# A Mamba layer and a position-attention layer: silu of z applied when the gate is loaded, a new order for the first image, and other shares of the scan's products for ScalarE, VectorE and GpSimd

## The chip, the cores and the metric

The kernel runs on one core of one Trainium2 chip. The metric is the device time of one execution in microseconds (us). Before the change it was measured three times: 3,081.79, 3,085.72 and 3,090.05 us, with a median of 3,085.72 us. One more execution was profiled, and its trace is read here.

A core has five engines, each with its own queue of instructions: TensorE (PE in the profile; its weight loads are PEld), VectorE (DVE), ScalarE (ACT), GpSimd (POOL) and SyncE (SP), which here only starts transfers between the chip's main memory (DRAM) and the on-chip memory. Matmuls write into PSUM[...], here used in tiles of 128 x 512 float32.

## What is computed

Input x is 4 x 512 x 32 x 32 in float32. Two layers follow each other. The first is a Mamba layer on the group-normalised x, with 1,024 inner channels, 16 states for each, and 1,024 time steps for each of four images:

```python
xz = xn @ W_in
xm, z = (xz[..., :d_inner], xz[..., d_inner:])
xc = jax.lax.conv_general_dilated(xm.transpose(0, 2, 1), conv_w[:, None, :], (1,), [(D_CONV - 1, 0)], ...)
xs = jax.nn.silu((xc + conv_b[None, :, None]).transpose(0, 2, 1))
proj = xs @ W_x
dt = jax.nn.softplus(proj[..., :dt_rank] @ W_dt + b_dt)
Bm = proj[..., dt_rank:dt_rank + D_STATE]
Cm = proj[..., dt_rank + D_STATE:]
A = -jnp.exp(A_log)

def step(h, inp):
    dt_t, B_t, C_t, x_t = inp
    dA = jnp.exp(dt_t[..., None] * A)
    h = dA * h + (dt_t * x_t)[..., None] * B_t[:, None, :]
    y = jnp.einsum('bds,bs->bd', h, C_t)
    return (h, y)
...
y = ys.transpose(1, 0, 2) + xs * D_param
y = y * jax.nn.silu(z)
out = y @ W_out
```

Here xn is the layer-normalised input. The result is added to x. The second layer group-normalises that sum again and computes two 1x1 convolutions (64 channels each), a softmax over their 1,024 x 1,024 products, a 3x3 convolution with 512 channels weighted by that softmax, and another 3x3 convolution with 512 channels. Its result is added too. All is float32.

## The kernel before

**Layer 0, units and groups.** Channels lie on the 128 partitions, time along the row. A *unit* is one state s of one pair of channel chunks (e, 256 channels) in one half of the time (h, 512 steps) of one image (b). Sixteen units make a *group*, eight groups an image, and there are 32 groups. For each unit (`unit`, line 814 on):

- ScalarE computes the decay exp(dt * A), line 832, two calls of 128 x 512.
- dt * x * B is formed in one of two ways. For s in `B_ON_ACT` (nine of sixteen) ScalarE scales the transposed dt * x by B (`sc`, line 844, four calls of 128 x 256) and TensorE transposes the result back into the PSUM ring `u` (line 870, eight transposes). For the other seven, GpSimd multiplies by a B row that a transfer has spread over the partitions (`dbx`, line 859, 128 x 1024).
- VectorE runs the scan along time (line 884, two of 128 x 512), and in the first half of the time stores the last state (line 889).
- The state is multiplied by C: on GpSimd (line 906, 128 x 1024), or for s in `C_ON_DVE` (four of sixteen) on VectorE (line 900, two of 128 x 512).
- TensorE adds the product over s, transposed, into y (line 913, eight instructions).

A group begins with `delta` (dt with its softplus, line 785; dt * x on GpSimd, line 793) and ends with `gate`: ScalarE copies y out of PSUM (line 936), TensorE turns it back, VectorE adds D * x and multiplies by silu(z).

**What lies between the groups.** The next image is prepared inside the groups of the present one: `norms` (statistics and normalisation), `conv1` (input projection, first tap on ScalarE line 639, three more on VectorE line 648, silu line 657), `gates` (projection of z, its silu at line 711, then a store to DRAM; `gate` loads it again), `params` (B, C and the input of dt), and `out_proj` of the image before. `transform`, called 32 times, turns the weights of the two 3x3 convolutions into the form that layer 1 uses: 12 additions on GpSimd each (lines 1173 to 1193), two scalings on ScalarE and 12 stores. For the first image `norms(0)` and `conv1_half` come before everything: the convolution is made half by half, with the last three columns of the first half kept in `tails` for the second (lines 676, 682, 687).

**What sets the order.** Nothing in layer 0 is issued where it is written. Each piece of work is recorded as a `Step` with its engine, an estimated duration, its reads and writes, a priority in units (`prio`), the activation table it needs (`table`), and the buffers that it takes from rings (`slots`: four `u` banks, four `h`, four `dbx` and so on). `Plan.issue` (line 106) keeps a clock for each engine, picks the step that can start first, breaks near ties by priority, charges 1.3 us (`LOAD`) when a step's table isn't the one loaded, and calls the step's function, which emits the instructions. So each engine has a fixed order, and priorities such as `PRM["dl"]` (how many units ahead `delta` comes), `m0`, `q0`, `c0`, `g0` or `tg` (distance of the transforms) decide it. The tables themselves are not loaded by the kernel: an instruction that needs another table gets a load (ACT_TABLE_LOAD) ahead of it when the kernel is compiled. Layer 0 has tables "exp", "ln", "silu" and "softplus".

**The end of layer 0 and layer 1.** The last image's gated y stays on chip; `last_proj` adds its output projection in parts, the last part after the last group. `first_image` loads image 0 for layer 1 and normalises it. Layer 1 is written in order: `scores` (matmuls `pt`, line 1324, and `psc`, line 1345), `conv3` (matmuls `m_b` and `m_o`, line 1468, whose operands `v` VectorE forms in lines 1453 to 1456 from `rr`), `attend` (matmuls `pat`). A scheduler chooses here in which order matmuls of different parts stand on TensorE.

## Time and profile before

| what | value |
|---|---|
| median of three runs | 3,085.72 us |
| the profiled execution | 3,085.98 us |
| its span, first to last instruction | 3,084.2 us |
| granted TensorE clock, mean | 0.967 |
| end of group 0 (its y copied, line 936) | 241.9 us |
| end of groups 7, 15, 23, 31 | 667.0, 1,147.6, 1,629.6, 2,044.5 us |
| first matmul of layer 1 (line 1324) | 2,058.3 us |

The profile gives for each engine the time in which it was busy, the idle time before groups of instructions, and what ended it (the releaser, an arrow). A table of windows gives, for stretches of the span in microseconds: their length, the busy time of TensorE's matmuls, of its weight loads, of VectorE, ScalarE and GpSimd (each with the number of instructions), the granted TensorE clock, the busy share of the transfer engines, and GB/s. The group view gives for each line of the program the count, the busy time in us, the mean duration in ns, and the idle time before. A line of the timeline begins with the start and the duration in us. A float32 matmul shows as two records, one per pass.

From 0 to 100 us VectorE is busy for 36.6 us and ScalarE for 40.0. Over the 32 groups every engine is busy for some nine tenths of the time. From about 2,060 us on layer 1 runs, in which TensorE is busy for 958.3 of the 984 us from 2,100 to 3,084.

### The profile page before, as it was taken

The page shows a single profiled execution, that of the slowest core. Times are in us where ns is not written, and L with a number is a line of the kernel's source. Part 1 is how long each engine was busy: PE and PEld are TensorE (multiplying, and loading weights), DVE is VectorE, ACT ScalarE, POOL GpSimd, SP SyncE. Part 2 cuts the span into 40 slices and gives each one's busy share as a digit, 9 for nine tenths or more (in the row PEclk, how much of TensorE's full clock was granted, in tenths as well). Part 3 has the DMA queues.
Part 4 walks back from the last instruction along what each step waited for, and adds up shares of the span by engine and source line. Part 5 has one row for each costly group of instructions (what it writes and reads, how often), then busy time and mean ns, then how long its engine had stood idle before and what let it go on. Part 6 is the DMA issues. An engine that isn't in the chain of part 4 may idle for free. (4 is left out here: it accounts for less than half of the span.)

```text
span 3084.2 us, 36053 instructions
## 1 busy us (share of the span) xinstructions
PE 2760.5 (90%) x11512; PEld 1625.3 (53%) x11512; DVE 2325.2 (75%) x3021; ACT 1864.1 (60%) x3218; POOL 2181.5 (71%) x1221
## 2 busy tenths in 40 slices
PE   4788789999879999879999978779999999999998
PEld 2245556656656666656656656544444444444444
DVE  3567999989999988999999899986275375447344
ACT  4578899998789999779999787741120030021000
POOL 6899988899988899998899999862151142224222
PEclk8899899999989999988999999999999999999999
DMA  6776645578745567755557755638178448628827
GB/s 170 216 208 197 178 143 164 171 210 255 230 138 163 165 204 238 236 176 158 174 167 238 237 184 151 148 123 307 54 259 314 163 165 315 256 76 313 309 86 259
DMA packets 410292, 610.49 MB, mean 198 GB/s; under 512 B 47832, under 2 KB 246744, under 8 KB 385528
## 3 DMA queue, kind: packets, MB, share of 16 engines
q1 hardware_dynamic: 401296, 593.67, 61.1%
q10 hardware_dynamic: 8648, 14.26, 1.3%
q8 instruction: 92, 1.51, 0.2%
q14 instruction: 96, 0.79, 0.1%
q0 software_dynamic: 160, 0.26, 0.0%
HBM read 511.09 MB, written 96.99 MB: 197 GB/s over the span
## 5 line engine op out<-in xcount | busy, mean ns | idle before, releaser
L906 POOL TENSOR_TENSOR da<-da,cbc 128x1024 f32<-128x1024 f32 x288 | 680.6, 2370 | 80.4 <-DVE da L884 50.7
L844 ACT ACTIVATE sc<-dtxt,bt_sb 128x256 f32<-128x256 f32 x1152 | 506.6, 497 | 70.6 <-PE u L870 70.1
L859 POOL TENSOR_TENSOR dbx<-dtx,bbc 128x1024 f32<-128x1024 f32 x224 | 529.1, 2373 | 20.1 <-PE y L913 7.0
L832 ACT ACTIVATE da<-dt,a_sb 128x512 f32<-128x512 f32 x576 | 395.4, 712 | 45.7 <-PE y L913 42.9
L884 DVE TENSOR_TENSOR_SCAN da<-da,carry_sb,u 128x512 f32<-128x512 f32 x288 | 357.6, 1263 | 34.5 <-PE u L870 34.5
L870 PE MATMUL u<-ident,sc 128*128 128x128 f32 x2304 | 345.8, 284 | 41.1 <-DVE da L884 26.0
L913 PE MATMUL y<-ident,da 128*128 128x128 f32 x2304 | 317.3, 282 | 53.2 <-POOL da L906 50.7
L913 PEld LDWEIGHTS y<-ident,da 128*128 128x128 f32 x2304 | 269.3, 145 | 155.6 <-POOL da L906 104.5
L884 DVE TENSOR_TENSOR_SCAN da<-da,u 128x512 f32<-128x512 f32 x288 | 348.6, 1210 | 2.6 <-PE u L870 2.4
L1468 PE MATMUL m_b<-uw_b,v_b 128*128 128x512 f32 x768 | 336.3, 595 | 8.8 <-DMA uw_b<-u_b 7.7
L870 PEld LDWEIGHTS u<-ident,sc 128*128 128x128 f32 x2304 | 277.2, 146 | 122.8 <-DVE da L884 34.7
L1468 PE MATMUL m_o<-uw_o,v_o 128*128 128x512 f32 x768 | 334.2, 595 | 4.3 <-DVE v_o L1387 4.1
L832 ACT ACTIVATE u<-dt,a_sb 128x512 f32<-128x512 f32 x448 | 297.6, 680 | 47.3 <-DVE da L884 27.6
L913 PE MATMUL y<-ident,dbx 128*128 128x128 f32 x1792 | 267.8, 289 | 61.2 <-DVE dbx L900 31.0
L913 PEld LDWEIGHTS y<-ident,dbx 128*128 128x128 f32 x1792 | 219.2, 149 | 135.0 <-issue 48.0
L394 PE MATMUL pxm<-xt,winc 128*128 128x345 f32 (+3 forms) x704 | 249.4, 498 | 29.3 <-DMA winc<-in_w_in_dram 12.9
L394 PE MATMUL pz<-xt,winc 128*128 128x512 f32 x512 | 240.3, 601 | 8.4 <-ACT sz L707 2.1
L1468 PEld LDWEIGHTS m_b<-uw_b,v_b 128*128 128x128 f32 x768 | 143.2, 190 | 195.0 <-issue 174.5
L1468 PEld LDWEIGHTS m_o<-uw_o,v_o 128*128 128x128 f32 x768 | 145.3, 190 | 190.1 <-issue 181.3
L906 POOL TENSOR_TENSOR dbx<-dbx,cbc 128x1024 f32<-128x1024 f32 x96 | 227.2, 2366 | 15.5 <-DVE dbx L884 7.5
L1518 PE MATMUL pat<-y_b,st 128*128 128x512 f32 x512 | 221.7, 593 | 0.1
L1476 ACT ACTIVATE e_b<-m_b 128x512 f32<-128x512 f32 x24 | 14.3, 597 | 307.9 <-PE m_b L1468 306.3
(233 smaller groups left out, 4543.1 us busy)
## 6 DMA issues: line engine op xcount, KB each, us to landing
cbc<-bcd SPq DMA_DIRECT2D x512, 256.0 KB, 3.7
uw_b<-u_b SPq DMA_DIRECT2D x96, 1024.0 KB, 5.1
uw_o<-u_o SPq DMA_DIRECT2D x96, 1024.0 KB, 4.8
bbc<-bcd SPq DMA_DIRECT2D x224, 256.0 KB, 3.9
u_b<-work SPq DMA_DIRECT2D x192, 128.0 KB, 2.7
u_o<-work SPq DMA_DIRECT2D x192, 128.0 KB, 3.3
winc<-in_w_in_dram SPq DMA_DIRECT2D x72, 256.0 KB, 3.6
szd<-sz SPq DMA_DIRECT2D x32, 512.0 KB, 4.1
```

The lines of the kernel that those rows point to most:

```text
L394: lambda k=k, lhs=lhs, rhs=rhs: nc.tensor.matmul(p()[:, at : at + cols], lhs(), rhs(), start=(k == 0), stop=(k == n - 1)),
L832: nc.scalar.activation(t, dt()[:, j], AF.Exp, scale=a_sb[:, at : at + 1])
L844: nc.scalar.activation(sc()[:, k], dtxt()[:, k], AF.Copy, scale=bt[:, at, s : s + 1])
L859: lambda: nc.gpsimd.tensor_mul(hc(), dtx(), b_bc().to_broadcast([P, 2, T])),
L870: nc.tensor.transpose(u()[:, k * P : (k + 1) * P], sc()[:, k, j, :], ident)
L884: nc.vector.tensor_tensor_scan(ht, *((hc()[:, j], u()) if on_act else (u(), hc()[:, j])), carry_sb[:, j, s : s + 1] if h else 0.0, ALU.mul ...
L906: lambda: nc.gpsimd.tensor_mul(hc(), hc(), c_bc().to_broadcast([P, 2, T])),
L913: nc.tensor.matmul(y[j]()[:, k, :], hc()[:, j, k * P : (k + 1) * P], ident, start=(s == 0 and k == 0), stop=(s == NS - 1 and k == NK - 1), ...
L1468: nc.tensor.matmul(m[q], v[:, q, k, c, :], w[:, c, :], start=(c == 0), stop=(c == NCC - 1 and not extra),)
L1476: nc.scalar.activation(e, m[2], AF.Copy, scale=al / 2)
L1518: nc.tensor.matmul(pt, st[m][:, 2 * P * j + h : 2 * P * (j + 1) : 2], xb[m // 2][:, m % 2, :], start=(m == 0), stop=(m == NMC - 1),)
```

## The change

The change has several parts, all in layer 0 and its order:

1. **silu of z.** `gates` stores z as it is. The silu is applied when the gate is loaded (`load_gate`, on the tile `szl`), inside the step that computes the softplus of the next group: `delta` takes a list `jobs`, whose functions are called before the softplus. The silus of the next image's convolution join the same list, two chunks at a time. So a group has one visit to the silu table, one to the softplus table, and then the exponential's again. `gate` of a group is recorded after `delta` of the next (`end_group`).
2. **Tables.** Ln, which had a table of its own in the plan, shares the exponential's: `exp_set` loads a set that has both, by hand, whenever the plan goes back to "exp".
3. **The first image.** x is loaded before anything else except one small matrix; the two halves are normalised one after the other, with more buffers for the squares; `conv1_half` and its `tails` are replaced by `conv1_first`, which uses the same `conv_part` as the other images and projects three columns of the first half again. The transforms come after the first projections by priority.
4. **Shares of the products.** Ten B products of sixteen go by ScalarE and TensorE, eleven in the last image. In the last image VectorE makes two C products instead of four, and GpSimd the others.
5. **Distances.** `dl` 10.28 to 8.5, `t0` 11 to 7 and `tg` 21.42 to 18.5 (the transforms), `m0`, `e0` and the convolution of image 1, and the new `zl` and `f1`.

```diff
-PRM = dict(..., m0=45.7, n0=50.77, nl=2.05, q0=65.56, qg=5.2, ..., e0=3.46, ..., dl=10.28, t0=11, tg=21.42)
+PRM = dict(..., m0=48, n0=50.77, nl=2.05, ..., e0=6, ..., dl=8.5, t0=7, tg=18.5, zl=11.5, f1=1.5)
...
-            s.fn()
             if late:
                 t += self.LOAD
                 table = s.table
+                if table == "exp":
+                    self.exp_set()
+            s.fn()
...
+    def exp_set():
+        nc.scalar.preload_act_table_set("natural_log_exp_and_others")
+
+    exp_set()
...
+        first_x = xtp.tile([P, NCC, L], F32, tag="xt", name="xt_0", bufs=1)
+        for c in range(NCC):
+            nc.sync.dma_start(first_x[:, c, :], x[0, c * P : (c + 1) * P].rearrange("p h w -> p (h w)"))
...
-        B_ON_ACT = (0, 2, 4, 6, 8, 10, 12, 14, 15)
-        C_ON_DVE = (1, 5, 9, 13)
+        B_ON_ACT = [(0, 2, 4, 6, 7, 8, 10, 12, 14, 15)] * (B - 1) + [(0, 2, 3, 4, 6, 8, 10, 11, 12, 14, 15)]
+        C_ON_DVE = [(1, 5, 9, 13)] * (B - 1) + [(5, 13)]
...
+            at_half = [prio + (lag * h if b else 0.5 * h) for h in range(NH)]
...
+                    if b:
+                        sq = buf("res", [P, T], f"sq_{b}_{h}_{c}")
+                        sqt = lambda sq=sq: sq()
+                    else:
+                        if c % 2 == 0:
+                            sq = buf(("dt", "dtx")[h], [P, 2, T], f"sq_{b}_{h}_{c}")
+                        sqt = lambda sq=sq, c=c: sq()[:, c % 2]
...
+        def silu(b, ds, hs=slice(0, L)):
+            hh = [h for h in range(NH) if hs.start < T * (h + 1) and hs.stop > T * h]
+            def each():
+                for d in ds:
+                    u = xs[b, d]()[:, hs]
+                    nc.scalar.activation(u, u, AF.Silu, bias=cb_sb[:, d : d + 1])
+            return (
+                each, len(ds) * (0.1 + 0.94 * len(hh) / NH), [xh[b, d][h] for d in ds for h in hh],
+                [xs[b, d] for d in ds],
+            )
...
+        def conv1_first(d, h, prio):
             if h == 0:
                 new_xs(0, d)
...
+            w = load_win(0, d, prio)
+            for at, end in (((0, T),), ((T, 768), (768, L)))[h]:
+                conv_part(0, d, w, at, end, prio, h == 0)
...
-            step(
-                "ACT", 0.97, lambda: nc.scalar.activation(sz(), sz(), AF.Silu),
-                [], [sz], prio, "silu",
-            )
...
-        def delta(b, e, h, prio):
+        def delta(b, e, h, prio, jobs=()):
...
+            def softplus():
+                for fn, *_ in jobs:
+                    fn()
+                nc.scalar.activation(dt(), dt(), AF.Softplus)
...
+        def load_gate(b, e, h):
+            prio = (b * NDC + 2 * e + h) * NS + NS
+            hs = halves[h]
+            sz = szl[b, e, h] = buf("szl", [P, 2, T], f"szl_{b}_{e}_{h}")
+            step(
+                "SP", 0.3, lambda: nc.sync.dma_start(sz(), szd[b][e][:, :, hs]),
+                szds[b][2 * e : 2 * e + 2], [sz], prio - PRM["zl"], kb=512,
+            )
+            return lambda: nc.scalar.activation(sz(), sz(), AF.Silu), 1.0, [sz], []
...
-            transform(u, src, k % NPC, -190 if k < PRM['t0'] else PRM['tg'] * (k - PRM['t0']))
+            transform(u, src, k % NPC, -5 if k < PRM['t0'] else PRM['tg'] * (k - PRM['t0']))
...
+                jobs = []
+                if b or n > 1:
+                    prev = b * NDC + n - 1
+                    jobs.append(load_gate(prev // NDC, prev % NDC // NH, prev % NH))
+                if b + 1 < B and n > 4:
+                    jobs.append(silu(b + 1, (2 * n - 10, 2 * n - 9)))
+                delta(b, e, h, at + n * NS - PRM["dl"] if b or n else -15, jobs)
+                end_group()
```

## The prediction

> **What bounds the kernel now.** I read the engine totals of the page first, then a table of windows, cut at the moments at which ScalarE copies a finished group's y (line 936), because the kernel is a chain of 32 such groups with a tail.
>
> ```profile
> PE 2760.5 (90%) x11512; PEld 1625.3 (53%) x11512; DVE 2325.2 (75%) x3021; ACT 1864.1 (60%) x3218; POOL 2181.5 (71%) x1221
> ```
>
> No engine stands out over the whole span, so the stages have to be looked at alone. The windows (us, busy PE, PEld, DVE, ACT, POOL):
>
> ```profile
> 0.00:100.00 100.00, 60.21 (x124) 24.85 (x124) 36.63 (x65) 40.04 (x67) 74.80 (x82) 0.90 0.64 179
> 200.00:241.90 41.90, 33.31 (x178) 22.08 (x177) 37.31 (x53) 36.20 (x64) 41.90 (x20) 0.94 0.61 183
> 721.06:777.69 56.63, 51.70 (x282) 35.98 (x280) 51.82 (x54) 45.07 (x86) 53.42 (x31) 0.97 0.84 261
> 894.56:968.31 73.75, 61.88 (x316) 44.22 (x315) 69.64 (x111) 67.79 (x110) 61.21 (x31) 0.93 0.50 150
> 1032.28:1096.24 63.96, 59.44 (x312) 38.97 (x311) 61.12 (x94) 62.36 (x107) 59.33 (x34) 1.00 0.60 176
> 1200.75:1259.02 58.27, 53.63 (x281) 36.34 (x279) 50.97 (x54) 47.27 (x86) 57.50 (x34) 0.94 0.82 266
> 1996.52:2044.48 47.96, 33.84 (x206) 24.56 (x207) 47.82 (x54) 25.49 (x50) 33.84 (x15) 0.96 0.52 139
> ```
>
> Three stages. Up to 241.9 us the first group is made; the vector engines idle most of the first 100. Then 31 groups take 1,802.6 us (2,044.5 - 241.9). In groups 1 to 3 of a batch POOL is full (57.5 of 58.3); in groups 5 to 7, where the next batch's convolution is interleaved, ACT and DVE are (62.4 and 61.1 of 64.0); at the very end DVE is (47.8 of 48.0). From 2,050 on layer 1 is TensorE's. The timeline of the start and of the crossing into layer 1:
>
> ```profile
> 24.00 0.16 DVE L476 SCALAR_TENSOR_TENSOR gnb_l<-gmean_l,pv_l 128x4 f32<-128x4 f32 x1 [2.47 <-ACT pv_l L463]
> ...
> 62.05 15.97 PE L394 MATMUL pxm<-xt,winc 128*128 128x512 f32 x32 [11.48 <-DMA winc<-in_w_in_dram]
> ...
> 114.89 2.49 POOL L793 TENSOR_TENSOR dtx<-dt,xs 128x512 f32<-128x512 f32 x2
> ...
> 2068.37 13.97 PE L1345 MATMUL psc<-center,top 128*128 128x512 f32 x32 [1.31 <-issue]
> ...
> 2075.77 1.25 DVE L1453 TENSOR_TENSOR v_b<-rr_b 128x1024 f32<-128x1024 f32 x1
> ```
>
> The statistics of the first image reach DVE at 24.00, after 2.47 us on ScalarE's Ln and Exp. The first projection (pxm) starts only at 62.05: before that TensorE waits 11.48 us for a weight load that stands behind transform stores on SP's queue. The first dtx is at 114.89. The table loads, by the groups view:
>
> ```profile
> L832 ACT ACT_TABLE_LOAD x76 | 97.5, 1283 | 1.4
> L785 ACT ACT_TABLE_LOAD x32 | 41.1, 1283 | 0.6
> L711 ACT ACT_TABLE_LOAD x28 | 35.9, 1283 | 0.5
> L657 ACT ACT_TABLE_LOAD x24 | 30.8, 1283 | 3.3 <-DVE xs L648 2.6
> ```
>
> **What the Trainium skill says.** "ScalarE: Activation LUTs", section What ACT_TABLE_LOAD costs, gives about 1283 ns for the load and about 1380 ns of drain on top. The trace has the 1283 ns, but the softplus load at 251.82 begins 0.01 us after the exponentials and the softplus 0.02 us after the load: no drain shows, so I price a load at 1.283 us. Its section Table sets: the hidden batching unit says that natural_log_exp_and_others has both exp and ln; no row of before shows it (Ln and Exp have a load each, lines 458 and 463). "PSUM — Partial Sum Buffer", section Engine vs sequencer instructions: queues are strict FIFO, and matmuls start in program order; the trace agrees (pxm above waits and everything behind it too). This carries the last part below.
>
> **The change, part by part.** Counts are from the order of the built programs.
>
> Table loads: 189 to 111, since silu of z moves into the step of the softplus of the next group, silus of the convolution join it, and Ln shares the exponential's set. 78 x 1.283 = 100 us less on ACT. Ten (last batch eleven) B products instead of nine: 40 more units on ACT, 160 sc activations. Alone they take 497 ns, back to back 0.44 (four in 1.71): +70 to +80 us. So ACT keeps 20 to 30 us, but the loads go mostly from groups 5 to 7 (28 loads in 894.56 to 1096.24, 3.2 groups, about 9 per group, against 3 after), where ACT binds; the products come everywhere.
>
> POOL: 40 B products fewer, 16 C products more (last batch four to two on DVE: 2 x 8). -24 x 2.37 = -57 us. DVE: 32 products fewer, 32 x 0.675 = -22 us, all in the last batch, and the little tail taps (line 687, 20.6 us) go in group 0. PE: 320 transposes more (four in 0.44): +35 us, nowhere the largest engine.
>
> Steady state. I counted, for each group and engine, the work that stands in program order between two group ends, with durations from the rows (issue to issue: POOL product 2.33, scan 1.235, sc 0.44, exp 0.63, load 1.283, matmul of 512 columns 0.86, four transposes 0.44), and took the largest engine of each group. For before this gives, for groups 1 to 7 of batch 0 and then batches 1, 2, 3: 419.3 + 472.4 + 472.6 + 425.6 = 1,789.9 us, and the trace has 425.1 + 480.6 + 482.0 + 414.9 = 1,802.6: within 1%. So the model may be used. For after: 413.0 + 463.5 + 465.0 + 428.0 = 1,769.5. The difference, **-20 us**, is small because the next engine is close: in the sixth and seventh group of batch 1 ACT falls from 62.3 and 64.1 to 54.8 and 56.3, but DVE stays at 60.7 and 59.2. In the last batch POOL takes over (its 2 x 8 more C products eat its saved B products, and four transforms instead of three lie there). The sums over all 31 groups say the same: largest engine 1,696 (DVE) before, 1,678 (POOL) after. What it could cost: the joined silu and softplus now hold ACT in one piece: 3 x 1.283 + 2 x 1.06 = 6.0 us, with two conv silus (1.15 each) 8.3 us, where a softplus alone took 3.6 us. Behind it stand the exponentials and sc of the next units, and the four u banks carry DVE over two units (5 to 7 us). Bounds: 0 lost to 20 lost; I take 0 beside the -20, since in before all waits of scans for exponentials (lines 884 after 832) came to about 27 us in 32 groups.
>
> Start. Five edits act together. x is loaded first: stats end about 3 us earlier, but a_sb (ready at 18.1, its multiply stands in DVE's queue) leaves some of it; Ln and Exp lose a load: mw about 3.6 us earlier. The halves go one after the other: the first half's mean takes 8 matmul passes (0.61 each, 4.9) instead of 16, then 2.7 (DVE), squares and variance to about 37.8, Ln and Exp 1.2, scaling 2.7 and affine 0.7: first projection at about 43 instead of 62.05, with winc already loaded. Eight projections at about 4 us and the eight parameter matmuls: proj copy at about 83 (100.4 before); copies, softplus with its load: 89.5. POOL has five transforms ahead of dtx (12.2 us each from about 21.4, with waits for ACT's scaling in between): dtx at 90 to 96 instead of 114.9. From there POOL still has 4 x 12.2 + 18 x 2.33 + 2.5 = 93 us up to the end of group 0 (113 before, which took 124.5 with its waits). With 11 to 13 us of waits: 95 + 105 = about 198 against 241.9. **-44 us**, bounds -30 (winc waits on SP, group 0 waits more) and -57 (no new waits). The three transforms that group 0 no longer holds (12 to 9) are in the steady sums already.
>
> Layer 1. Its order stays, but for one thing: the first matmul of m_b0 now stands before psc in TensorE's queue. It needs v_b's first plane, made by line 1453, which ends at 2077.0; psc started at 2068.37. FIFO then holds psc back. In after the output projection is no longer split by pt, so v_b comes 1.7 us earlier against it: 2077.0 + 0.9 - 1.7 - 68.4 = **+8 us**; bounds +3 (if the two rr_b sums, 3.6 us each beside POOL and 1.29 alone in other rounds, run fast) and +10. Layer 1's own Ln and Exp loads (6) lie where ACT idles: 0, hidden by the pat matmuls.
>
> Sum against the profiled execution's own 3,086.0 us (span 3,084.2), which is the median shown (3,085.7) within 0.3: 3,086 - 44 - 20 + 8 = **3,030 us**.
>
> **Rivals.** (B) The joined blocks take back the steady gain: 3,086 - 44 + 8 = 3,050. For: they are twice as long. Against: ACT has 3 to 8 us of slack per group after. (C) More than that: with ACT relieved the groups lose their 1% over the largest engine (13 us), group 0 waits 6 us less, and v_b is early (+3): 3,086 - 50 - 33 + 3 = 3,006. (D) Slower: one mechanism, DVE and POOL run dry behind each joined block. The place is ACT's queue at each softplus, 31 times, the price the excess over 3.6 us: 22 x 2.4 + 9 x 4.7 = 95 us; 3,030 + 95 = 3,125. It decides once a block starves the others for (44 + 20 - 8)/31 = 1.8 us. Against it: u and h rings carry two units, and projections and copies lie around. (E) The start doesn't gain, because POOL's transforms, not x, set it: 3,086 - 10 - 20 + 8 = 3,064. Against: the 11.48 us wait for winc and 16 passes in the way are real.
>
> **How the numbers follow.** Likeliest 3,030: 0.58, own range 3,015 to 3,045. B 0.17, C 0.12, E 0.06, D 0.06, no change 0.01. 0.3% of the time, 9 us, is about what a measurement of this kernel can tell from no change. Faster: 0.58 + 0.17 + 0.12 + 0.06 = 0.93, less a little of E: 0.92; slower 0.06; same 0.02. The range 3,000 to 3,060 holds the first three and leaves out D, E and the outer bounds.
>
> **What would show it.** First pxm near 43, proj near 83, first y copy near 198; 111 table loads; groups 5 to 7 of batches 1 and 2 at 60 to 62 with DVE full and ACT at 55; the last batch near 415 with POOL full; psc waiting about 8 us behind an m_b matmul that waits for v_b. Wrong if scans wait for exponentials for over 50 us in all, or if the first y copy stays beyond 215.

## The result, and the profile after

The changed kernel takes 3,077.7 us (median of 18 runs, 3,073.0 to 3,088.5), the kernel before, measured beside it, 3,079.8: a ratio of 0.9992, with a 95% interval from 0.9983 to 1.0001. No change is clear of the noise; 3,030 was predicted. The profiled execution has a span of 3,077.3 us. Cut at the same moments as before (ScalarE's copy of a finished group's y, now line 948), it divides as follows:

| stretch | before, us | after, us | change | predicted |
|---|---|---|---|---|
| up to the end of the first group | 241.9 | 198.0 | -43.9 | -44 |
| 31 groups | 1,802.6 | 1,835.0 | +32.4 | -20 |
| last y copy to the end (layer 1) | 1,039.7 | 1,044.3 | +4.6 | +8 |

The start and layer 1 came as worked out. The 31 groups in the middle should have become 20 us shorter and became 32 us longer: 53 us are missing there. The page's engine totals and the chain that ended last:

```profile
PE 2789.0 (91%) x11896; PEld 1669.4 (54%) x11896; DVE 2290.1 (74%) x2989; ACT 1822.0 (59%) x3300; POOL 2125.4 (69%) x1197
...
PE 40%; DVE 12%; ACT 6%; DMA 4%; POOL 4%; issue 3%; SPq 0%; DVEq 0%; POOLq 0%; ACTq 0%
```

VectorE, ScalarE and GpSimd all have less work than before (2,325.2, 1,864.1 and 2,181.5 us then), and TensorE has 28.5 us more. So for those three the amount of work doesn't explain the longer groups. The chain doesn't settle it either: it can be followed back over 69% of the span here, and before only over 44%. The granted TensorE clock was the same in the 31 groups, 0.96 before and after. The table loads did what was said (76 + 32 + 28 + 24 on the four lines shown before, with the rest 189; now 41 + 32 + 32 + 6):

```profile
L206 ACT ACT_TABLE_LOAD x41 | 52.6, 1283 | 3.1 <-issue 1.7 <-PEq L1681 0.7
L786 ACT ACT_TABLE_LOAD x32 | 41.1, 1283 | 0.5
L935 ACT ACT_TABLE_LOAD x32 | 41.1, 1283 | 0.5
L675 ACT ACT_TABLE_LOAD x6 | 7.7, 1283 | 1.9 <-DVE xs L661 1.9
```

The table of windows of after (stretch; us, busy PE, PEld, DVE, ACT, POOL with counts; granted clock, DMA share, GB/s): the fifth to eighth group of batch 1 and the fourth group of the last batch (a batch is an image).

```profile
859.42:931.68 72.26, 63.46 (x324) 44.02 (x323) 69.55 (x109) 63.72 (x112) 56.52 (x33) 0.98 0.49 138
931.68:996.57 64.89, 59.95 (x326) 41.82 (x325) 58.47 (x73) 53.38 (x98) 55.98 (x33) 1.00 0.56 167
996.57:1059.47 62.90, 57.27 (x314) 40.30 (x313) 60.55 (x95) 54.75 (x96) 58.88 (x34) 1.00 0.58 176
1059.47:1115.95 56.48, 56.24 (x299) 33.23 (x298) 45.11 (x48) 51.12 (x97) 49.66 (x30) 1.00 0.68 196
1771.17:1834.30 63.13, 41.09 (x248) 30.98 (x247) 44.21 (x43) 48.23 (x91) 59.45 (x35) 0.84 0.52 164
```

In the sixth group (64.89 us) nothing is full: DVE has 58.47, PE 59.95. The same view of before, for the sixth and the eighth group of batch 1 (the seventh stands in the prediction), has ACT close to full in the sixth and PE full in the eighth:

```profile
968.31:1032.28 63.97, 58.48 (x309) 41.59 (x308) 60.18 (x75) 61.35 (x101) 53.07 (x29) 0.95 0.57 161
1096.24:1147.56 51.32, 51.32 (x282) 32.75 (x282) 44.32 (x47) 48.02 (x83) 49.32 (x28) 1.00 0.65 198
```

ScalarE lost 8 us in the sixth and in the seventh group (61.35 to 53.38, 62.36 to 54.75), as predicted, and the groups lasted 0.9 us more and 1.1 us less. Idle time took the place of the work. Much of it shows in VectorE's waits, between the end of the first group and the last y copy (waiting line, what it waited for: us in total, times, longest). First of before, then of after:

```profile
DVE da L884 <- PE u L870: 36.9, 33, 3.1
DVE dbx L884 <- ACT u L832: 17.8, 16, 2.4
...
DVE da L889 <- PE u L875: 62.5, 35, 13.2
DVE dbx L889 <- ACT u L837: 50.1, 15, 7.5
```

In each pair the first line is a scan that waits for dt * x * B, transposed by TensorE, and the second one that waits for a decay in u (below: VectorE's wait for u). The prediction had set a mark here: wrong if scans wait for exponentials for over 50 us. Counted over all lines in which a scan waits for one, as the prediction had counted its 27 us, it is 26.7 us before and 56.2 after. One such wait in full, the timeline of after in the sixth group of batch 1 (start, us, engine, line, operation, in square brackets the idle time ahead and its releaser):

```profile
963.86 1.28 ACT L935 ACT_TABLE_LOAD   x1
965.15 1.06 ACT L935 ACTIVATE szl<-szl 128x1024 f32<-128x1024 f32 x1
966.12 2.17 ACT L675 ACTIVATE xs<-xs,cb_sb 128x1024 f32<-128x1024 f32 x2
968.31 1.28 ACT L786 ACT_TABLE_LOAD   x1
969.60 1.06 ACT L786 ACTIVATE dt<-dt 128x1024 f32<-128x1024 f32 x1
970.57 0.89 ACT L849 ACTIVATE sc<-dtxt,bt_sb 128x256 f32<-128x256 f32 x2
971.37 0.56 ACT L709 COPY sz<-pz 128x512 f32<-128x512 f32 x1
971.83 0.91 ACT L849 ACTIVATE sc<-dtxt,bt_sb 128x256 f32<-128x256 f32 x2
972.64 0.57 ACT L709 COPY sz<-pz 128x512 f32<-128x512 f32 x1
973.23 1.28 ACT L206 ACT_TABLE_LOAD   x1
974.52 1.30 ACT L837 ACTIVATE u<-dt,a_sb 128x512 f32<-128x512 f32 x2
...
975.25 2.46 DVE L889 TENSOR_TENSOR_SCAN dbx<-u,carry_sb,dbx 128x512 f32<-128x512 f32 x2 [4.84 <-ACT u L837]
```

From the first load at 963.86 to the next decay (the exponential of dt) at 974.52 are 10.66 us. The prediction had priced 8.3: it had left out that the plan sets table-free work (sc, copies of z) between softplus and the load back to the exponential, which lengthens the time without decays by 2.4 us. VectorE has nothing to scan from 970.41 on and stands for 4.84 us. I call such a time, from the first table load away from the exponentials to the next decay, a *stretch*; it is added up below from each kernel's ScalarE timeline over the 31 groups.

### The profile page after: what moved, and what is told of

It reads as the page before. It is cut to its first block, busy times and chain, and to the rows that moved or that the text cites. A ratio compares the mean times of both kernels' runs of the same rounds, so it can differ in the third digit from the quotient of the medians.

```text
span 3077.3 us, 36921 instructions
## 1 busy us (share of the span) xinstructions
PE 2789.0 (91%) x11896; PEld 1669.4 (54%) x11896; DVE 2290.1 (74%) x2989; ACT 1822.0 (59%) x3300; POOL 2125.4 (69%) x1197
## 4 chain that ended last, share of the span: by engine, by line
PE 40%; DVE 12%; ACT 6%; DMA 4%; POOL 4%; issue 3%; SPq 0%; DVEq 0%; POOLq 0%; ACTq 0%
PE m_o L1503 10%; PE m_b L1503 8%; PE pat L1553 7%; DVE da L889 5%; PE y L918 3%; PE po L402 2%; PE psc L1380 2%; PE u L875 2%; DMA uw_b<-u_b 2%; POOL da L911 2%; DVE dbx L889 2%; DVE u L889 1%; PE pz L402 1%; PE pp L728 1%; ACT sc L849 1%
## 5 line engine op out<-in xcount | busy, mean ns | idle before, releaser
L911 POOL TENSOR_TENSOR da<-da,cbc 128x1024 f32<-128x1024 f32 x328 | 773.2, 2368 | 114.7 <-DVE da L889 53.1
L849 ACT ACTIVATE sc<-dtxt,bt_sb 128x256 f32<-128x256 f32 x1312 | 578.1, 499 | 99.3 <-PE u L875 98.5
L837 ACT ACTIVATE da<-dt,a_sb 128x512 f32<-128x512 f32 x656 | 454.1, 716 | 78.8 <-PE y L918 62.8
L864 POOL TENSOR_TENSOR dbx<-dtx,bbc 128x1024 f32<-128x1024 f32 x184 | 434.4, 2373 | 10.6 <-DVE carry_sb L894 4.6
L918 PE MATMUL y<-ident,da 128*128 128x128 f32 x2624 | 366.6, 284 | 72.1 <-POOL da L911 69.9
L889 DVE TENSOR_TENSOR_SCAN da<-da,u 128x512 f32<-128x512 f32 x328 | 397.9, 1213 | 31.0 <-PE u L875 29.0
L402 PE MATMUL pxm<-xt,winc 128*128 128x341 f32 (+4 forms) x768 | 251.0, 470 | 21.7 <-DVE xs L661 10.5
L837 ACT ACTIVATE u<-dt,a_sb 128x512 f32<-128x512 f32 x368 | 245.5, 681 | 11.9 <-DVE da L889 6.7
L918 PE MATMUL y<-ident,dbx 128*128 128x128 f32 x1472 | 215.4, 285 | 36.0 <-DVE dbx L905 24.7
L661 DVE SCALAR_TENSOR_TENSOR xs<-pxm,cw_sb,xs 128x341 f32<-128x341 f32 (+8 forms) x288 | 163.6, 569 | 60.6 <-ACT xs L652 53.6
```

Of the source, the lines that this page charges most:

```text
L402: lambda k=k, lhs=lhs, rhs=rhs: nc.tensor.matmul(p()[:, at : at + cols], lhs(), rhs(), start=(k == 0), stop=(k == n - 1)),
L661: nc.vector.scalar_tensor_tensor(u()[:, first:end], p()[:, first - k - at + before : n - k + before], cw[k], u()[:, first:end], ALU.mult, ...
L837: nc.scalar.activation(t, dt()[:, j], AF.Exp, scale=a_sb[:, at : at + 1])
L849: nc.scalar.activation(sc()[:, k], dtxt()[:, k], AF.Copy, scale=bt[:, at, s : s + 1])
L864: lambda: nc.gpsimd.tensor_mul(hc(), dtx(), b_bc().to_broadcast([P, 2, T])),
L889: nc.vector.tensor_tensor_scan(ht, *((hc()[:, j], u()) if on_act else (u(), hc()[:, j])), carry_sb[:, j, s : s + 1] if h else 0.0, ALU.mul ...
```

## The experiments

Theory 1, after the first reading: the long stretch starves VectorE and, through it, the others. Its rivals: the new shares cost the time (2), the parameter products pile up in the last group of a batch (3), the transforms that left the first group are just paid back later (4). Times are medians; ratios are to the kernel before, measured beside each on the same chip. Stretches, waits and the lengths of groups are from the profiled execution.

### First four: undo one part each

**e1_conv_alone.** The silus of the convolution leave the joined block:

```diff
-                if b + 1 < B and n > 4:
-                    jobs.append(silu(b + 1, (2 * n - 10, 2 * n - 9)))
...
-                    alone(silu(b + 1, range(6, NDC)), at + PRM["c0"] + PRM["cg"] * NDC)
...
             for at, end in ((0, 341), (341, 682), (682, L)):
                 conv_part(b, d, w, at, end, prio)
+            alone(silu(b, (d,)), prio)
```

> The changed kernel with the convolution silus of batches 1 to 3 taken out of the blocks in front of softplus: each stands alone after its own channel group, as before; silu of z stays joined. Groups 5 to 8 of batches 0 to 2 took 777.8 us in the changed kernel (755.5 before). Theory 1, the long joined block starves VectorE and TensorE: those twelve groups come to about 755, VectorE's scans wait for u under 25 us in all instead of 50, and the time falls to about 3,055. Theory 2, the shares (ten B products, last batch) cost it: nothing returns, 3,078 plus up to 24 table loads of 1.28 us, to 3,095. Theory 3, the parameter products pile up in the last group of a batch behind the last silus: only the last group of batches 0 to 2 falls, by 5 us each, to 3,063.

Measured: 3,071.0 us, ratio 0.9975 [0.9964, 0.9986]. The 31 groups take 1,828.3 us, 6.7 less; VectorE's wait for u 39.3 us; the fifth to eighth groups of batches 0 to 2 come to 776.9 us instead of 777.6. Within these the eighth groups fall (171.0 to 161.3), which fits theory 3; the others rise by 9.0 together, while 35 table loads come back in the 31 groups (135 instead of 100). A small gain, far from what theory 1 expected of this part.

**e2_all_alone.** That, and silu of z back at the projection of z:

```diff
                     [p], [sz], prio,
                 )
+            step(
+                "ACT", 0.97, lambda: nc.scalar.activation(sz(), sz(), AF.Silu),
+                [], [sz], prio, "silu",
+            )
...
-                    jobs.append(load_gate(prev // NDC, prev % NDC // NH, prev % NH))
+                    load_gate(prev // NDC, prev % NDC // NH, prev % NH)
```

> As the last one, and silu of z too as before: computed at the gate's projection, before it is stored, with no job in front of softplus. The start, Ln and Exp in one table, the shares and the transforms stay as changed. Theory 1: the 31 groups fall from 1,835.0 to below the 1,802.6 of before, by what the shares bring, to near 1,790, and the time to about 3,035; ScalarE's table loads rise by 60 to 70 us and cost nothing. Theory 2 or 4 (transforms paid back later): the 31 groups stay at 1,825 to 1,845 and the time at 3,070 to 3,090. If only the conv silus matter it equals the last run within 5 us.

Measured: 3,080.0 us, ratio 1.0003 [0.9993, 1.0014]; 31 groups 1,835.7 us. Theory 1 in its first form fails: with no silu joined in the program nothing is won. The stretches didn't go, though: the plan sets lone silus next to softplus, and there are 70 stretches of 6.58 us on average (35 of 7.66 in after). But something did move. VectorE's wait for u fell from 50.1 to 15.0 us (all waits of scans for exponentials from 56.2 to 37.5), and ScalarE is full again in groups in which it had been before. So I made the prediction's sum (the largest engine of each group, from the order of the built program) for every kernel here:

| kernel | sum of the largest engines | 31 groups measured | more than the sum |
|---|---|---|---|
| before | 1,790 | 1,803 | 13 |
| after | 1,769 | 1,835 | 66 |
| e1, convolution silus alone | 1,775 | 1,828 | 53 |
| e2, all silus alone | 1,810 | 1,836 | 26 |

The sums are estimates; for the kernel before the sum is 13 us off, and differences of that size between kernels mean little. By this estimate, joining the silus takes 41 us out of the sum and adds 40 us to what comes more: the table loads saved and the longer blocks would cancel, hence no difference between e2 and after. That is an account by the sum; this run doesn't show it by itself.

**e3_shares.** The shares of before:

```diff
-        B_ON_ACT = [(0, 2, 4, 6, 7, 8, 10, 12, 14, 15)] * (B - 1) + [(0, 2, 3, 4, 6, 8, 10, 11, 12, 14, 15)]
+        B_ON_ACT = [(0, 2, 4, 6, 8, 10, 12, 14, 15)] * B
-        C_ON_DVE = [(1, 5, 9, 13)] * (B - 1) + [(5, 13)]
+        C_ON_DVE = [(1, 5, 9, 13)] * B
```

> The changed kernel with the shares of before in all batches: nine B products on ScalarE and PE, four C products on VectorE. Theory 2, the shares cost it: the 31 groups fall from 1,835.0 to about 1,800 and the time to about 3,045. Theory 1: POOL's 24 products come back (57 us over the batches, a third of it in the way), so the 31 groups take 1,835 to 1,855 and the time is 3,078 to 3,098; VectorE's waits for u stay near 50 us.

Measured: 3,111.5 us, ratio 1.0109 [1.0094, 1.0124]; 31 groups 1,885.6 us, 50.6 more than after. Theory 2 is out: the shares are worth 34 us of time (the first group is 5.7 us shorter without them and layer 1 8.7), more than either theory gave them; their sum says 32 for the 31 groups. Without them the change would be a clear loss.

**e5_transforms.** t0=11 and tg=21.42 instead of 7 and 18.5.

> The changed kernel with the weight transforms at their old places (eleven ahead of the first scans instead of seven, the rest further apart). Theory 4, the start's gain is paid back where the transforms now stand: the first group gets longer by up to 36 us and the 31 groups shorter by as much, so the time stays within 5 us of 3,078. Theories 1 and 2: POOL has idle time in the steady state except in the last batch, so the start loses 20 to 36 us, the 31 groups win 10 at most, and the time is 3,090 to 3,110.

Measured: 3,099.8 us, ratio 1.0072 [1.0057, 1.0087]. The first group ends at 237.7 (39.7 later) and the 31 groups take 1,819.9 (15.1 less). Theory 4 is out as the cause: three transforms moved out of the first group win 40 there and cost 15 later. It also says that nearly all of the start's 44 us hang on these transforms: with them at their old places the first group ends 4.2 us earlier than before.

### Next three: the last batch, the block's place, the block's length

**e4_last_batch.** Only the shares of the last batch as in the others (ten B products; four C products on VectorE).

> The changed kernel with the last batch's shares as in the other batches (ten B products on ScalarE instead of eleven, four C products on VectorE instead of two). The last batch took 427.2 us (414.9 before), its fourth group 63.1 (48.5 before) with POOL full. Theory A, the two C products moved to POOL made POOL the bound: the last batch falls by about 10 us to 417 and the time to 3,068. Theory B, the transform that now stands in the fourth group did it: that group stays at 58 us or more and the time within 4 us of 3,078.

Measured: 3,068.8 us, ratio 0.9962 [0.9947, 0.9977]. The last batch takes 421.7 us (427.2), and its fourth group 54.1 instead of 63.1, still full on POOL by the table of windows, with less to do there (53.59 us, after 59.45):

```profile
1763.52:1817.58 54.06, 39.75 (x242) 30.04 (x241) 45.81 (x48) 45.97 (x84) 53.59 (x32) 0.91 0.58 185
```

So theory A's forecast holds for that group: the last batch's shares cost it 9 us, and other groups of the batch give some of this back. Layer 1 is 5.0 us shorter here too, so the 9 us of time are not the shares' alone. And theory B is not out. e5 keeps after's shares but has no transform in that group, and there the group takes 48.6 us and the last batch 409.2, 18 less than in after:

```profile
1812.57:1861.16 48.59, 41.22 (x264) 31.36 (x263) 46.06 (x48) 47.53 (x89) 48.59 (x23) 0.96 0.57 193
```

The twelve additions of the transform take 12.0 us of POOL in after's fourth group, its twenty products some 47. Both together make POOL the bound there; taking away either shortens the group.

**e6_dl.** dl=10.28 instead of 8.5: the step times of a group, with the joined block, come earlier in the group ahead.

> The changed kernel with each group's step times and its joined silus due 10.28 units ahead of the group, as before, instead of 8.5. Theory P, the place of the block matters (dt and dtx come late): VectorE's waits for u and POOL's for dt fall, the 31 groups take 1,815 or less. Theory L, the length of the stretch in which ScalarE makes no decay matters wherever it stands: the waits of VectorE for u stay at 40 to 60 us and the 31 groups within 8 us of 1,835.

Measured: 3,070.4 us, ratio 0.9967 [0.9957, 0.9977]; 31 groups 1,820.8 us, 14.2 less; VectorE's waits for u fall from 52.1 to 16.4 us in all (scans that write u included), but those for transposed u (line 875) rise from 62.5 to 80.4. That is about midway between the two forecasts: place matters, but the waits partly change their name. The stretches are shorter too (mean 7.24 us, after 7.66).

**e7_exp_ln.** Softplus from two functions of the decays' own table, so that only the silus need another one:

```diff
-            def softplus():
+            def silus():
                 for fn, *_ in jobs:
                     fn()
-                nc.scalar.activation(dt(), dt(), AF.Softplus)
...
+            if jobs:
+                step(
+                    "ACT", sum(j[1] for j in jobs), silus,
+                    [], [t for j in jobs for t in j[2]], prio, "silu",
+                    holds=[t for j in jobs for t in j[3]],
+                )
+            step("ACT", 1.06, lambda: nc.scalar.activation(dt(), dt(), AF.Exp), [], [dt], prio, "exp")
+            step("ACT", 1.06, lambda: nc.scalar.activation(dt(), dt(), AF.Ln, bias=1.0), [], [dt], prio, "exp")
```

> The changed kernel with softplus computed as Exp and then Ln(1 + .), which lie in the table of the decays, so that softplus needs no table; the silus of z and of the convolution stay joined in one silu block. The stretch without decays shrinks from 6.0 to 3.6 us, and in the groups with two convolution silus from 8.3 to about 5.8, while ScalarE's work in the 31 groups stays (1,609 us by the sum of its instructions, 1,621 as changed) and the sum of the largest engine of each group too (1,771 and 1,769). Theory L, the length of the stretch starves VectorE: its scans wait for u under 25 us instead of 50, the 31 groups fall by 20 to 40 us and the time to 3,040 to 3,058. If the stretch's length does not matter: within 6 us of 3,078.

Measured: 3,043.8 us, ratio 0.9882 [0.9867, 0.9896]. The 31 groups take 1,814.1 us, 20.9 less, with the sum of the largest engines unchanged (1,771). VectorE's waits of e7:

```profile
DVE da L891 <- PE u L877: 49.5, 38, 4.1
...
DVE dbx L891 <- ACT u L839: 12.7, 10, 2.9
```

50.1 us have become 12.7, and the longest wait for transposed u 4.1 instead of 13.2. So 21 us in the 31 groups go with the shorter block. The plan also ordered the other engines' work anew, so that this run alone doesn't show that the length did it. The rest of the 34 us is not that: the first group ends 9.3 us earlier (seven additions of a transform, 6.2 us of POOL, and one product fewer lie in it), and layer 1 is 7.3 us shorter (see below).

### Three more: a longer block, and combinations

**e8_longer.** The order of TensorE, VectorE and GpSimd exactly as in after, and two needless copies in each block:

```diff
                     fn()
                 nc.scalar.activation(dt(), dt(), AF.Softplus)
+                nc.scalar.copy(dt(), dt())
+                nc.scalar.copy(dt(), dt())
```

> The changed kernel with the block made longer and nothing else: two copies of dt onto itself (about 1 us each on ScalarE) behind each of the 32 softplus, every engine's order as it was. ScalarE's work grows by 64 us, 2 us a group, and stays below the largest engine in nearly all groups (it was 53 to 55 us of 63 to 65 in groups 6 and 7 of a batch). Theory L, the length of the stretch without decays is on the path: VectorE's waits for u grow from 50 to 80 us or more and the 31 groups by 30 to 60 us, to 3,108 to 3,138 in all. If ScalarE's idle time covers it: the time stays within 8 us of 3,078.

Measured: 3,144.8 us, ratio 1.0216 [1.0201, 1.0231]: 67 us more than after for about 64 us of copies, 60.9 of them in the 31 groups; that is above even theory L's range. This is the plainest run of the study, since nothing else was ordered anew. By busy time ScalarE is the largest engine in only 4 of the 31 groups (in after in one), the prediction's sum rises by 7 us only, and yet every microsecond goes through to the end. The waits of e8:

```profile
DVE dbx L891 <- ACT u L839: 84.9, 24, 8.5
DVE da L891 <- PE u L877: 72.9, 41, 17.0
...
POOL dtx L800 <- ACT dt L788: 55.5, 26, 4.2
```

VectorE waits 85 us for decays (after: 50.1) and GpSimd 55.5 us for dt (after: 12.8). So the block's length is on the path. Two ways lead from it, which this run doesn't separate: the copies keep decays from VectorE, and, since they write dt, they also hold back dt itself, on which GpSimd's dt * x waits. Copies of another tile would have told them apart; none was run. In after itself the wait for decays is the larger of the two.

**e10_exp_ln_last** is e7 with e4's shares of the last batch:

> Softplus as Exp and Ln, and the last batch's shares as in the other batches: each alone took 34 and 9 us from the changed kernel's time. If they are separate causes, as theory L and the POOL-bound last batch say: 3,035. If the last batch's 9 us was the block's starvation again: 3,044.

Measured: 3,044.4 us, ratio 0.9888 [0.9870, 0.9906]. The last batch takes 424.5 us (e7: 425.9), so almost nothing of e4's gain is left with the shorter block; layer 1 is 6 us longer. The two don't add up. What part of e4's 9 us was starvation was not separated further.

**e9_exp_ln_last_dl** is e10 with dl=10.28:

> The last kernel with the step times due 10.28 units ahead of their group instead of 8.5, which alone took 7 us. Theory L: the short block no longer starves VectorE, so that its place brings 5 us at most (3,030 to 3,037). Theory P, the place matters by itself: 3,028 or less.

Measured: 3,027.7 us, ratio 0.9838 [0.9824, 0.9853], the best version of the study, about 50 us below both kernels. 31 groups: 1,796.7. That is at the edge of theory P's forecast: the place brings 17 us even with the short block. The timeline of e9, in the sixth group of batch 1, shows through what:

```profile
932.29 1.28 ACT L937 ACT_TABLE_LOAD   x1
933.58 1.06 ACT L937 ACTIVATE szl<-szl 128x1024 f32<-128x1024 f32 x1
934.54 2.17 ACT L675 ACTIVATE xs<-xs,cb_sb 128x1024 f32<-128x1024 f32 x2
936.62 0.56 ACT L816 COPY dtxt<-pdt 128x512 f32<-128x512 f32 x1
937.09 0.54 ACT L652 ACTIVATE xs<-pxm,cw_sb 128x342 f32<-128x342 f32 x1
937.65 1.28 ACT L206 ACT_TABLE_LOAD   x1
938.94 1.30 ACT L839 ACTIVATE u<-dt,a_sb 128x512 f32<-128x512 f32 x2
```

6.65 us from load to decay, where after had 10.66 with the same three silus: one load and the softplus are gone, and less other work has slipped in ahead of the load back. Over the kernels with joined silus and the new shares (after, e6, e7 and e8 with those of the last batch), the 31 groups follow the stretches; e5, with fewer transforms in these groups, is left out (34 stretches, 260 us, 1,819.9 us):

| kernel | stretches | mean, us | sum, us | 31 groups, us |
|---|---|---|---|---|
| e9 | 34 | 5.37 | 182 | 1,796.7 |
| e10 | 34 | 6.45 | 219 | 1,814.5 |
| e7 | 34 | 6.58 | 224 | 1,814.1 |
| e6 | 35 | 7.24 | 253 | 1,820.8 |
| e4 | 35 | 7.48 | 262 | 1,825.9 |
| after | 35 | 7.66 | 268 | 1,835.0 |
| e8 | 35 | 9.41 | 329 | 1,895.9 |

From after to e8 a microsecond of stretch costs one of time (61 for 61); from e7 to after half of one (21 for 44). The table says nothing of kernels with other shares or with the silus apart: before has 75 stretches of 5.42 us on average, 407 us in all, and e2 460 us, more than any here. What is counted is how these runs go together; only e8 changed the stretch and nothing else.

### Last two: is joining needed, and what would Exp and Ln alone bring

**e11_exp_ln_alone** is e9 with the edits of e1 and e2 (no silu joined).

> The kernel with softplus as Exp and Ln, the last batch's shares as in the others and the 10.28 units, and now with no silu joined to another: each stands alone as before the change. Its table loads rise from 78 to 110, but no stretch without decays is longer than about 3.6 us. If only the stretch's length counts: 3,028, as with joined silus. If the loads count as work in the groups in which ScalarE is full (the sum of the largest engines is 56 us higher, 1,816 and 1,760): 3,060 to 3,085.

Measured: 3,046.6 us, ratio 0.9897 [0.9875, 0.9918], between the two forecasts. With a short block, joining is worth 19 us. The expectation's premise didn't hold, however: the stretches are not all short, but 50 of 5.55 us on average and up to 11.5, 277 us in all (e9: 182). So whether the loads count as work (100 in the 31 groups instead of 68) or through the stretches is not separated.

**e12_before_exp_ln** is the kernel before with softplus from Exp and Ln, and nothing else.

> The kernel before, with softplus as Exp and Ln and Ln in the decays' table, and nothing else of the change. ScalarE's work in the 31 groups falls from 1,611 to 1,560 us, the sum of the largest engines by 4 us (1,790 and 1,786). If the stretch of 3.6 us around softplus (load, softplus, load) was covered in the kernel before: 3,076 to 3,082, and the shares and the start are what the version with Exp and Ln gains by. If it starved VectorE there too: 3,050 to 3,065.

Measured: 3,074.8 us, ratio 0.9986 [0.9979, 0.9993]: 5 us, and these lie in the start: the first group ends 8.1 us earlier, and the 31 groups take 1,805.9 us, 3.3 more than before. In the kernel before, the softplus block was covered; it is the changed kernel that gains by its removal.

## Why the prediction was wrong

**The step that failed** is in the part Steady state: "Bounds: 0 lost to 20 lost; I take 0 beside the -20", and the sum of the largest engine under it. About 53 us were lost, in every batch: what the 31 groups took more than the prediction's sum went from 5.8, 8.2, 9.4 and -10.7 us in the four batches before to 24.5, 17.0, 24.9 and -0.8 after. (The 1% by which the sum fitted before came in part from errors of both signs that cancel.) By place of the group in its batch, an estimate of what came more than the sum's change said, in after and in e7 with its shorter stretch:

| groups | after, us | e7, us |
|---|---|---|
| first, of batches 1 to 3 | 11.1 | 4.6 |
| fifth, of batches 0 to 2 | 10.7 | 2.1 |
| sixth | 7.9 | 3.4 |
| seventh | 13.6 | 9.8 |
| eighth | 4.1 | 4.7 |
| fourth of the last batch | 4.6 | 0.0 |
| all others | 1.4 | 6.2 |
| sum | 53.4 | 30.8 |

In plain lengths, the eighth groups of batches 0 to 2 grew by 14.4 us together and the fourth group of the last batch by 14.6; all others came to 3.4 more, where they should have become shorter.

Two things are in it. *First, the stretch.* The sum counts how much each engine has to do in a group and takes it that an engine with room to spare holds nobody up. The four u banks cover about two units, and the prediction said so ("5 to 7 us"); but it priced the blocks at 6.0 and 8.3 us and argued from ScalarE's slack per group. The trace has 7.66 us on average and 10.66 in the case shown. I read it so: slack ahead of the block helps only until the four banks are full, and slack behind it comes too late. No run varied the number of banks, so this part is argued. What the runs show: with a shorter stretch 21 us came back (e7) and, with its place and the last batch's shares changed as well, 38 (after to e9, in which the sum is 9 us lower too); lengthening it cost all of it (e8). *Second, mis-sized terms.* In the seventh groups the sum had ACT at 64.1 and DVE at 59.2 us before, so that relieving ScalarE seemed worth 5 us each. The window in the prediction itself has DVE at 61.12 busy of 63.96, beside ACT's 62.36: both were nearly full, and the group could shrink by about 1 us. The eighth groups are TensorE's, full before (51.32 of 51.32) and after (56.24 of 56.48), 5.2 us longer in batch 1 where the sum said 3.1. e1, in which fewer parameter products pile up there behind the last joined silus, takes 2.4 to 4.5 us from each.

How much of the 53 us each of the two makes stays open. The kernel before has long stretches too, 15 of over 7 us and up to 12.2 (after: 16), so that their length alone doesn't set after apart from it. VectorE's idle time that ends within a stretch or 1.5 us behind it is 67.7 us before, 91.1 in after, 34.7 in e7 and 146.3 in e8; by this, an estimate, stretches make some 23 of the 53 us. And e9 still runs about 37 us above its own sum, the kernel before 13.

**The start** was right in its terms. The timeline of after, with the crossing into layer 1 at the end:

```profile
40.34 7.13 PE L402 MATMUL pxm<-xt,winc 128*128 128x512 f32 x16
...
80.25 0.58 ACT L739 COPY proj<-pp 64x512 f32<-64x512 f32 x1 [1.84 <-PE pp L728]
...
92.04 2.50 POOL L798 TENSOR_TENSOR dtx<-dt,xs 128x512 f32<-128x512 f32 x2 [1.07 <-ACT dt L786]
...
2058.28 1.23 DVE L1488 TENSOR_TENSOR v_b<-rr_b 128x1024 f32<-128x1024 f32 x1
2059.61 2.04 PE L1503 MATMUL m_b<-uw_b,v_b 128*128 128x512 f32 x2 [8.30 <-issue]
2061.45 14.54 PE L1380 MATMUL psc<-center,top 128*128 128x512 f32 x32
```

Forecast were 43, 83 and 90 to 96 for the first three, and 198 for the end of the group (198.0). The first two came 3 us early, so that the fit of the last is in part luck. e5 adds what the prediction had in its sum but didn't say aloud: the gain hangs on POOL's transforms more than on x coming first. That was the premise of rival E.

**Layer 1** was right in its mechanism. The last lines show the m_b matmul ahead of psc, with 8.30 us of idle time before it, and psc behind it in the queue. The profile names no releaser ("issue"), but v_b's first plane ends at 2059.51 and m_b starts at 2059.61. That psc is held back with it is the in-order rule that the prediction took from the Trainium skill, "PSUM — Partial Sum Buffer", section Engine vs sequencer instructions. The net cost was 4.6 instead of 8. Since the order of these two varies among the kernels here while layer 1's text doesn't, they give a rough price once more: with m_b first (after, e1, e5, e6, e8) layer 1 takes 1,043.4 to 1,047.5 us, mean 1,044.6; with psc first (before, e2, e3, e4, e7, e9, e10, e11, e12) 1,035.6 to 1,043.0, mean 1,039.0. The means differ by 5.6 us, but the second set alone spreads over 7.4.

**The last batch** was predicted to grow by 2.4 us and grew by 12.3. e4 and e5 show the term: the fourth group's POOL, with 59.45 us of products and a transform. The prediction had both and still took 428.0 us for the batch; its sum for the kernel before, 425.6, was 10.7 too high there.

**The rivals.** B (the gain of the steady state taken back, 3,050) and D (VectorE and GpSimd run dry behind each joined block) had the mechanism. D's own point of decision, 1.8 us per group, is where the case came to rest: 53 us over 31 groups are 1.7. D was given 0.06 because the u and h rings carry two units and other work lies around. That is an argument, and no measurement excluded D; a loss between B's 20 us and D's full excess lay outside the range.

The Trainium skill, "ScalarE: Activation LUTs", section Table sets: the hidden batching unit, advises batching activations by table set. This case agrees where the batch stays short (e9 against e11: 19 us for 32 loads less) and shows the price where it doesn't (after against e2: 52 loads less in the 31 groups, no time gained). The set with exp and ln that the section names is shown by the timeline of e7: one load serves the Exp of dt, its Ln and the decays behind them.

```profile
947.60 1.28 ACT L206 ACT_TABLE_LOAD   x1
948.89 1.06 ACT L793 ACTIVATE dt<-dt 128x1024 f32<-128x1024 f32 x1
949.98 1.06 ACT L794 ACTIVATE dt<-dt 128x1024 f32<-128x1024 f32 x1
...
951.41 1.31 ACT L839 ACTIVATE u<-dt,a_sb 128x512 f32<-128x512 f32 x2
```

## What to carry to other kernels

An engine with idle time can still set the pace if it serves others in small portions and is then away from them for long (e8). Where that happens, compare its absences with what is buffered behind it, and not only its busy share with its neighbours'. Batch operations to save a switch only as far as that cover reaches, and see what else the scheduler lets slip into the absence. A function built from two that are in the table already loaded can be cheaper than one that needs its own: the changed kernel took 34 us less with it, orders that changed along included, but the kernel before gained nothing by it in its 31 groups.

## What was not expected of the hardware

TensorE's passes cost more where products with 64 output rows (the parameter products, 128*64 in the profile) stand between transposes, and not where products with 128 do. The timeline of after in the sixth group of batch 1, with projections of z, and in the eighth, with parameter products:

```profile
985.58 1.04 PE L918 MATMUL y<-ident,da 128*128 128x128 f32 x8
986.45 1.02 PE L402 MATMUL pz<-xt,winc 128*128 128x512 f32 x2
987.31 0.60 PE L875 MATMUL u<-ident,sc 128*128 128x128 f32 x4
...
1070.28 1.09 PE L918 MATMUL y<-ident,da 128*128 128x128 f32 x8
1071.30 1.07 PE L728 MATMUL pp<-xs,wx_sb 128*64 128x512 f32 x2
1072.30 1.09 PE L918 MATMUL y<-ident,dbx 128*128 128x128 f32 x8
```

From start to start, eight transposes take 0.87 us ahead of the projection and 1.02 ahead of the parameter product; two passes of the projection take 0.86 us and two of the parameter product 1.00. Over the 31 groups of after the medians are the same: 0.86 us for 49 such pairs of the projection, 1.00 for 33 of the parameter products. So each such pair costs some 0.3 us more between transposes. In a group in which TensorE is full, spreading the parameter products costs that much each time. Why is not shown.

And ScalarE's switch of tables again cost its 1,283 ns and no more: in the timeline of the sixth group above, the load at 968.31 begins 0.02 us after the last silu ends, and softplus 0.01 us after the load; the further 1,380 ns of drain that the Trainium skill gives ("ScalarE: Activation LUTs", section What ACT_TABLE_LOAD costs) do not show.
